# A graph layer in split single precision on one core: small tiles get a pool of their own ahead of the large ones

## The chip, the cores and the metric

The kernel runs on one core of one Trainium2 chip. The metric is the time of one execution in microseconds (us), as the device measures it; each kernel is run several times and the median counts.

## The reference

For each of 64 graphs with 256 nodes and 768 features the reference normalizes the features, takes the positive part `h`, and adds a graph layer to the input:

```python
h   = jnp.maximum(_layernorm(x, axis=-1), 0.0)
adj = heads.astype(hs.dtype);  radj = jnp.swapaxes(adj, 1, 2)
deg_c, rdeg_c = row sums of adj and radj, zeros replaced by 1
ctx = jnp.matmul(adj, hs @ Wadj.T + badj) / deg_c[..., None]
ctx = ctx + jnp.matmul(radj, hs @ Wrev.T + brev) / rdeg_c[..., None]
ctx = ctx + hs @ Wself.T + bself
rel = terms of the relation table E, gathered by adj and summed per node
out = x + ctx + rel
```

The heavy part is `h` (16,384 rows of 768) times three matrices of 768 x 768, and then the two aggregations with the adjacency matrix. All of it is in single precision.

## The kernel before

**The work.** The product of a graph's `h` with the three weight matrices is a product of a 2 x 3 by a 3 x 3 grid of blocks (two halves of the nodes, three parts of the features, three matrices). The kernel does it in 15 block products by fixed linear combinations (the tables `PRODUCTS` and `SWEEPS`), in two sweeps over the graphs: eight products (chains y, z and w) for all graphs first, then seven (chains x, v, u and t). Partial results go to DRAM between the sweeps. The first and the last graph are done with plain products (`whole`, L782).

**One product.** Its precision comes from splitting each operand into words of the format fp32r. The right operand (combined weights) is split once per sweep into three tiles `word{n}_0..2`, which stay in SBUF for all graphs. The left operand (a combination of parts of the transposed `h`) is split for each graph into one tile `left` of three words (`split`, L600 to L617). `passes` (L628) then issues matmuls of 128 x 128 by 384 columns: `left` is the stationary operand, loaded anew for each matmul, and `word` is the moving operand. A product has 12 such passes, in a run of eight and a run of four or the other way round, with a ScalarE operation on the PSUM bank between them (`scale`, L666). In the second sweep each graph also has four aggregations of eight passes (`aggregate`, L944), with `a` (the adjacency matrix) stationary and the pair `hl` (a block split in two words) moving.

**The order.** Nothing is ordered by hand. `record` writes down every operation with a rank, and `Plan.schedule` plays them through with estimated durations, engine by engine, and gives each buffer a slot of its class when it is first needed. The classes are W (24 slots of 6144 bytes in each partition: words, raw weights, `hl`), B (18 of 3072: `left`, `h`, blocks, rows), T (5 of 1024), A (3 of 4096: `adj`, `a`, some `x`), S (6 small ones: statistics, transposed statistics, diagonals), and Q and U in PSUM. The order and the slots come from the estimates alone; addresses play no part in them. Which slot a given `left`, `hl` or `a` gets changes from graph to graph.

**The addresses.** Each slot is one tag of the tile pool `pool`, and the pool lays its tags out in the order in which they first come up; a tag is as large as its largest tile, rounded up to 32 bytes. The constants end at byte 1248 of each partition. Then come, in the same pool, the tiles made by `own` (L1088): `deg` 1024 bytes, `sq` 512, two `cols` and two `tokens` of 512 each, two `rd` of 16. Then come the slots, in order of first use, so that S slots lie between W and B slots:

```
from byte  mod 256   what lies there
  1248       224     deg, sq, cols, tokens, rd
  4896        32     B B B W W
 26400        32     S (96 bytes), S (128 bytes)
 26624         0     W B A B W W B W W W
 76800         0     S (512 bytes), S (512 bytes)
 77824         0     B W W B B B B W W W B B W B W B W
154624         0     S (128 bytes)
154752       128     A B B A W B W W W W W W W
221312       128     S (512 bytes)
221824       128     T T T T T
226944               end
```

Within a tile the matmul operands start at multiples of 512 bytes from the tile's start.

The lines that the change touches are the definition of `own` (L1088) and the choice of a pool for a slot (L1109), both in `main_path`.

Of the kernel before, what the change touches and what calls it, by code (L numbers as in the profile page):

```python
# [1041 lines left out]
def kernel(  # L1042
# [34 lines left out]
    flag = const.tile([1, 1], I32, name="flag")  # L1077

    def main_path(main: ExitStack):
        pool = main.enter_context(tc.tile_pool(name="pool", bufs=1))  # L1080
        dram = main.enter_context(tc.tile_pool(name="dram", bufs=3, space=bass.MemoryType.DRAM))
        keep = main.enter_context(tc.tile_pool(name="kept", bufs=1, space=bass.MemoryType.DRAM))
        psum = main.enter_context(tc.tile_pool(name="psum", bufs=1, space=bass.MemoryType.PSUM))
        singles = ExitStack()
        single = singles.enter_context(tc.tile_pool(name="single", bufs=1, space=bass.MemoryType.PSUM))
        held, late = None, None
        plan = Plan(SLOTS)
        own = lambda name, shape, dtype: plan.buf(None, shape, dtype, name, pool.tile(shape, dtype, name=name))  # L1088
        fixed = {
            "x": x_v, "xt": x_t, "adj": adj_v, "out": out_v, "e_t": e_t, "bias": bias,  # L1090
            "w": (wadj_t, wself_t, wrev_t), "wr": (wr_t, wrr_t),
            "ident": ident, "ones": ones, "half": half, "dram": dram, "kept": keep,
            "flag": plan.buf(None, None, None, "flag", flag),
            "deg": own("deg", [P, B, C, 2], F32),
            "sq": own("sq", [P, B, C], F32),
            "cols": [own(f"cols{i}", [P, P], F32) for i in range(2)],
            "tokens": [own(f"token{i}", [P, P], F32R) for i in range(2)],
            "rd": [own(f"rd{i}", [P, C, 2], F32) for i in range(2)],
        }
        for col in fixed["cols"]:  # L1100
            nc.vector.memset(col.tile, 0.0)
        nc.scalar.activation(half[:, :1], half[:, :1], AF.Copy)
        record(nc, plan, fixed, B, NREL)
        for o in plan.schedule():
            for b in o.bufs:
                if b.name == "hold":
                    held = b.slot
                elif b.tile is None:
                    home = {"Q": psum, "U": single}.get(b.cls, pool)  # L1109
                    if b.cls == "Q" and b.slot == held:  # L1110
                        if late is None:
                            singles.close()
                            late = main.enter_context(tc.tile_pool(name="late", bufs=1, space=bass.MemoryType.PSUM))
                        home = late
                    b.tile = home.tile(b.shape, b.dtype, tag=f"{b.cls}{b.slot}", name=b.name)
            o.emit()
# [123 lines left out]
    with ExitStack() as main:  # L1240
        with tc.manual_schedule():
            main_path(main)
# [37 lines left out]
```

## Time and profile before

| | before |
|---|---|
| median of 3 runs | 2497.23 us (2497.17 to 2497.82) |
| the profiled execution | 2496.79 us |
| its span, first to last instruction | 2495.0 us |
| TensorE busy | 2468.1 us, 13,858 matmuls |
| VectorE, ScalarE, GpSimd busy | 2098.2, 1781.8, 1285.4 us |
| share of 16 DMA engines, main queue | 68.8% |

The profile is of one execution. Busy time is the union of an engine's instructions. A line number is that of the kernel before. A matmul's record lasts longer than its turn, since matmuls are pipelined: the pace of a run is read from its start to the start of what follows it.

### The profile page before, as it was taken

The page shows a single profiled execution, that of the slowest core. Times are in us where ns is not written, and L with a number is a line of the kernel's source. Part 1 is how long each engine was busy: PE and PEld are TensorE (multiplying, and loading weights), DVE is VectorE, ACT ScalarE, POOL GpSimd, SP SyncE. Part 2 cuts the span into 40 slices and gives each one's busy share as a digit, 9 for nine tenths or more (in the row PEclk, how much of TensorE's full clock was granted, in tenths as well). Part 3 has the DMA queues.
Part 4 walks back from the last instruction along what each step waited for, and adds up shares of the span by engine and source line. Part 5 has one row for each costly group of instructions (what it writes and reads, how often), then busy time and mean ns, then how long its engine had stood idle before and what let it go on. Part 6 is the DMA issues. An engine that isn't in the chain of part 4 may idle for free.

```text
span 2495.0 us, 43288 instructions
## 1 busy us (share of the span) xinstructions
PE 2468.1 (99%) x13858; PEld 2386.0 (96%) x13858; DVE 2098.2 (84%) x4003; ACT 1781.8 (71%) x3772; POOL 1285.4 (52%) x1138
## 2 busy tenths in 40 slices
PE   6999999999999999999999999999999999999999
PEld 4899999999999999996999999999999999999998
DVE  7887888788788778868988888888888888888887
ACT  4788888888888888876666666666666666666665
POOL 1555555555555555543555555555555555555554
PEclk9999999999999999999999999999999999999999
DMA  5677777777777777776666666666666666666663
GB/s 214 245 282 279 267 271 279 275 266 279 278 269 273 281 270 272 291 252 215 221 213 213 213 214 214 210 216 215 212 211 211 213 215 213 215 214 213 213 217 134
DMA packets 224776, 590.66 MB, mean 237 GB/s; under 512 B 25080, under 2 KB 25080, under 8 KB 224544
## 3 DMA queue, kind: packets, MB, share of 16 engines
q1 hardware_dynamic: 224544, 587.86, 68.8%
q8 instruction: 110, 1.80, 0.3%
q14 instruction: 122, 1.00, 0.1%
HBM read 364.28 MB, written 223.48 MB: 236 GB/s over the span
## 4 chain that ended last, share of the span: by engine, by line
PE 97%; DVE 1%; DMA 1%; ACT 1%; issue 0%; POOL 0%; SPq 0%; ACTq 0%; POOLq 0%
PE x L628 21%; PE y L628 20%; PE agg L944 14%; PE z L628 10%; PE w L628 10%; PE t L628 5%; PE v L628 5%; PE u L628 5%; PE whole L782 2%; PE v L638 1%; DMA raw<-in_Wself_dram 0%; PE right L502 0%; PE pt L915 0%; DMA row<-d 0%; DVE right L555 0%
## 5 line engine op out<-in xcount | busy, mean ns | idle before, releaser
L932 POOL TENSOR_TENSOR hl<-c,hl 128x768 fp32r<-128x768 f32 x256 | 476.0, 1860 | 655.4 <-ACT hl L928 449.6
L628 PE MATMUL x<-word,left 128*128 128x384 f32 x2976 | 592.1, 340 | 0.2 <-DVE c L687 0.2
L628 PE MATMUL y<-word,left 128*128 128x384 f32 x2976 | 573.9, 337 | 0.1
L628 PEld LDWEIGHTS x<-word,left 128*128 128x128 f32 x2976 | 517.5, 188 | 14.1 <-issue 11.2
L628 PEld LDWEIGHTS y<-word,left 128*128 128x128 f32 x2976 | 522.9, 188 | 4.1 <-ACT y L666 1.0
L944 PE MATMUL agg<-hl,a 128*128 128x384 f32 x2048 | 399.1, 337 | 0.0
L944 PEld LDWEIGHTS agg<-hl,a 128*128 128x128 f32 x2048 | 361.9, 188 | 0.5 <-issue 0.2
L745 POOL TENSOR_TENSOR h<-h,row 128x768 f32<-128x768 f32 x128 | 235.2, 1859 | 172.5 <-DMA row<-d 138.6
L628 PE MATMUL z<-word,left 128*128 128x384 f32 x1488 | 301.3, 337 | 0.7 <-DVE x L793 0.4
L628 PE MATMUL w<-word,left 128*128 128x384 f32 x1488 | 301.5, 338 | 0.2 <-ACT w L666 0.2
L666 ACT ACTIVATE x<-x 128x768 f32<-128x768 f32 x248 | 191.8, 794 | 141.5 <-PE x L628 141.5
L628 PEld LDWEIGHTS w<-word,left 128*128 128x128 f32 x1488 | 264.1, 188 | 0.8 <-ACT w L666 0.7
L628 PEld LDWEIGHTS z<-word,left 128*128 128x128 f32 x1488 | 260.6, 188 | 3.8 <-DVE x L793 0.7
L955 DVE SCALAR_TENSOR_TENSOR c<-agg,rd,c 128x768 f32<-128x768 f32 x252 | 255.2, 1013 | 8.5 <-PE agg L944 4.2
L928 ACT ACTIVATE hl<-c 128x768 fp32r<-128x768 f32 x256 | 215.1, 841 | 30.3 <-DVE c L685 24.4
L666 ACT ACTIVATE y<-y 128x768 f32<-128x768 f32 x248 | 197.0, 794 | 42.4 <-PE y L628 41.4
L722 POOL TENSOR_TENSOR cols<-cols,half 128x2 f32<-128x2 f32 x64 | 83.1, 1298 | 259.3 <-DVE cols L721 259.3
L617 DVE SCALAR_TENSOR_TENSOR left<-left,top 128x256 fp32r<-128x256 f32 x496 | 199.8, 414 | 6.4
L685 DVE TENSOR_TENSOR c<-c,v 128x768 f32<-128x768 f32 x124 | 117.4, 947 | 104.2 <-PE v L628 103.2
L617 DVE SCALAR_TENSOR_TENSOR left<-left 128x256 fp32r<-128x256 f32 x434 | 203.8, 492 | 0.1
L607 ACT ACTIVATE top<-left 128x256 f32<-128x256 f32 x496 | 180.8, 382 | 6.2 <-DVE left L617 2.1
L676 ACT ACTIVATE c<-y 128x768 f32<-128x768 f32 x124 | 100.9, 814 | 72.2 <-PE y L628 72.1
(136 smaller groups left out, 4320.1 us busy)
## 6 DMA issues: line engine op xcount, KB each, us to landing
c<-kept SPq DMA_DIRECT2D x316, 384.0 KB
kept<-c SPq DMA_DIRECT2D x252, 384.0 KB
x<-in_x_dram SPq DMA_DIRECT2D x128, 384.0 KB
h<-in_x_t_dram SPq DMA_DIRECT2D x128, 384.0 KB
out_dram<-c SPq DMA_DIRECT2D x126, 384.0 KB
kept_h<-h SPq DMA_DIRECT2D x124, 384.0 KB
h<-kept_h SPq DMA_DIRECT2D x124, 384.0 KB
adj<-in_adj_dram SPq DMA_DIRECT2D x64, 512.0 KB
```

The costliest lines, as they stand in the source:

```text
L607: lambda: nc.scalar.activation(view(top), t(w)[:, 0].bitcast(F32), AF.Copy),
L617: lambda: nc.vector.scalar_tensor_tensor(t(w)[:, 2], t(w)[:, 1].bitcast(F32), -STEP, first(), op0=ALU.mult, op1=ALU.add), s == 1,
L628: nc.tensor.matmul(t(q)[:, half, : H // 2], t(w)[:, lw, f, :], t(r[rw])[:, f, ts(half, H // 2)], start=start and i == 0 and f == 0, stop=s ...
L666: lambda: nc.scalar.activation(view(), view(), AF.Copy, scale=scale),
L676: lambda o=o, sign=sign: nc.scalar.activation(t(o).rearrange("p (k n) -> p k n", k=2), view(), AF.Copy, scale=sign * (1.0 if value_last el ...
L685: emit = lambda to=to, op=op: nc.vector.tensor_tensor(to(), to(), view(), op=op)
L722: pool(0.7, r - 21.5, f"pow {b}", [col], [col], lambda: nc.gpsimd.tensor_tensor(var(), var(), v["half"], op=ALU.pow))
L745: lambda h=h, one=one: nc.gpsimd.tensor_tensor(t(h), t(h), one(0), op=ALU.subtract),
L928: lambda: nc.scalar.activation(t(pair)[:, 0], t(o), AF.Copy, scale=LOWER),
L932: lambda: nc.gpsimd.tensor_tensor(t(pair)[:, 1], t(o), t(pair)[:, 0].bitcast(F32), op=ALU.subtract),
L944: nc.tensor.matmul(t(q)[:, half, : H // 2], t(s["a"])[:, c, k, ts(ic, P)], t(pairs[c])[:, part, ts(half, H // 2)], start=(c == 0 and part ...
L955: lambda q=q, to=to, ic=ic: nc.vector.scalar_tensor_tensor(to(), t(q)[:, :, : H // 2], t(rd)[:, ic, k : k + 1], to(), op0=ALU.mult, op1=AL ...
```

## The change

The tiles made by `own` and the S slots come from a second pool, `small`, which is opened ahead of `pool` and so lies ahead of it in each partition. Sizes, slots, operations and their order are the same.

```diff
     def main_path(main: ExitStack):
+        small = main.enter_context(tc.tile_pool(name="small", bufs=1))
         pool = main.enter_context(tc.tile_pool(name="pool", bufs=1))
...
-        own = lambda name, shape, dtype: plan.buf(None, shape, dtype, name, pool.tile(shape, dtype, name=name))
+        own = lambda name, shape, dtype: plan.buf(None, shape, dtype, name, small.tile(shape, dtype, name=name))
...
                 elif b.tile is None:
-                    home = {"Q": psum, "U": single}.get(b.cls, pool)
+                    home = {"Q": psum, "U": single, "S": small}.get(b.cls, pool)
```

## Rows read from the trace of the kernel before

**Rows 1.** The page, head and part 1: busy us, share of the span, instructions

```profile
span 2495.0 us, 43288 instructions
...
PE 2468.1 (99%) x13858; PEld 2386.0 (96%) x13858; DVE 2098.2 (84%) x4003; ACT 1781.8 (71%) x3772; POOL 1285.4 (52%) x1138
```

**Rows 2.** The page, part 4: the chain that ended last, share by engine

```profile
PE 97%; DVE 1%; DMA 1%; ACT 1%; issue 0%; POOL 0%; SPq 0%; ACTq 0%; POOLq 0%
```

**Rows 3.** Waits of TensorE: us in total, times, longest us

```profile
PE whole L782 <- DVE h L749: 18.9, 1, 18.9
PE pt L915 <- DVE x L793: 0.8, 1, 0.8
PE z L628 <- DVE x L793: 0.4, 1, 0.4
PE t L628 <- ACT t L666: 0.2, 1, 0.2
PE x L628 <- DVE c L687: 0.2, 1, 0.2
PE z L628 <- ACT z L666: 0.2, 1, 0.2
PE w L628 <- ACT w L666: 0.2, 1, 0.2
```

**Rows 4.** Busy time by stretch: first sweep, second sweep (columns in the first line)

```profile
core 0: us, PE busy (x) PEld busy (x) DVE busy (x) ACT busy (x) POOL busy (x), PEclk, DMA share, GB/s
100.00:1050.00 950.00, 949.92 (x5419) 945.96 (x5418) 759.99 (x1692) 796.59 (x1585) 525.12 (x511) 1.00 0.77 275
1200.00:2430.00 1230.00, 1230.00 (x7089) 1202.67 (x7089) 1086.31 (x1878) 793.69 (x1822) 642.34 (x529) 1.00 0.66 214
```

**Rows 5.** Groups by line, matmuls: xcount | busy us, mean ns | idle before

```profile
L628 PE MATMUL x<-word,left 128*128 128x384 f32 x2976 | 592.1, 340 | 0.2 <-DVE c L687 0.2
L628 PE MATMUL y<-word,left 128*128 128x384 f32 x2976 | 573.9, 337 | 0.1
...
L944 PE MATMUL agg<-hl,a 128*128 128x384 f32 x2048 | 399.1, 337 | 0.0
...
L628 PE MATMUL w<-word,left 128*128 128x384 f32 x1488 | 301.5, 338 | 0.2 <-ACT w L666 0.2
L628 PE MATMUL z<-word,left 128*128 128x384 f32 x1488 | 301.3, 337 | 0.7 <-DVE x L793 0.4 <-ACT z L666 0.2
...
L628 PE MATMUL t<-word,left 128*128 128x384 f32 x744 | 151.1, 338 | 0.2 <-ACT t L666 0.2
L628 PE MATMUL u<-word,left 128*128 128x384 f32 x744 | 150.7, 337 | 0.0
L628 PE MATMUL v<-word,left 128*128 128x384 f32 x744 | 150.2, 337 | 0.0
...
L782 PE MATMUL whole<-raw,h 128*128 128x384 f32 x288 | 97.3, 493 | 18.9 <-DVE h L749 18.9
```

**Rows 6.** Timeline of TensorE, two successive graphs: start us, us, what

```profile
1552.06 1.56 PE L944 MATMUL agg<-hl,a 128*128 128x384 f32 x8
1553.47 0.85 PE L628 MATMUL x<-word,left 128*128 128x384 f32 x4
1554.16 1.58 PE L628 MATMUL t<-word,left 128*128 128x384 f32 x8
1555.58 1.21 PE L628 MATMUL x<-word,left 128*128 128x384 f32 x6
...
1573.08 1.55 PE L944 MATMUL agg<-hl,a 128*128 128x384 f32 x8
1574.47 0.85 PE L628 MATMUL x<-word,left 128*128 128x384 f32 x4
1575.16 1.57 PE L628 MATMUL t<-word,left 128*128 128x384 f32 x8
1576.57 1.21 PE L628 MATMUL x<-word,left 128*128 128x384 f32 x6
```

**Rows 7.** Timeline of TensorE, the run of u in two graphs

```profile
1502.38 1.55 PE L628 MATMUL u<-word,left 128*128 128x384 f32 x8
1503.77 0.86 PE L628 MATMUL v<-word,left 128*128 128x384 f32 x4
...
1565.37 1.57 PE L628 MATMUL u<-word,left 128*128 128x384 f32 x8
1566.78 0.86 PE L628 MATMUL v<-word,left 128*128 128x384 f32 x4
```

**Rows 8.** Timeline of TensorE, runs of z and w in the first sweep

```profile
502.89 0.86 PE L628 MATMUL z<-word,left 128*128 128x384 f32 x4
503.59 1.57 PE L628 MATMUL w<-word,left 128*128 128x384 f32 x8
505.00 1.22 PE L628 MATMUL y<-word,left 128*128 128x384 f32 x6
...
519.73 0.87 PE L628 MATMUL z<-word,left 128*128 128x384 f32 x4
520.44 1.04 PE L628 MATMUL w<-word,left 128*128 128x384 f32 x5
...
1008.34 1.55 PE L628 MATMUL w<-word,left 128*128 128x384 f32 x8
1009.73 1.03 PE L628 MATMUL y<-word,left 128*128 128x384 f32 x5
```

## The prediction

> **What bounds the kernel.** I read the page's busy times first: TensorE is busy 2468.1 us of a span of 2495.0 us, 99%, and VectorE, the next, 84% [rows 1]. The reader is to see there that one engine fills the span. The chain of waits then has to confirm that this engine also sets the end, and it does: 97% of the chain is TensorE [rows 2]. The list of what TensorE waited for shows the slack in that: 18.9 us once, at the start, and less than 1 us for every other entry [rows 3]. The table by stretches says the same of the two long stages: TensorE is busy 949.92 of 950 us in the first (batches through the first sweep of products) and 1230.00 of 1230 us in the second, at a granted clock of 1.00, the 2.4 GHz level, while VectorE has 760 and 1086 us [rows 4]. So the time is a number of matmuls times the pace of one.
>
> How many: L628 issues 2976 + 2976 + 1488 + 1488 + 744 + 744 + 744 = 11,160 and L944 issues 2048, together 13,208 passes of 384 columns [rows 5]. How fast: the first stage has 949.92 us / 5419 = 175.3 ns for one [rows 4], and over the 12,923 of these passes that follow another one without a gap, start to start in the timeline, it is 175.2 ns. One nanosecond more or less in each is 13.2 us, half a per cent of the span. A change that only moves tiles can act here and nowhere else.
>
> **The change part by part.** It adds no instruction, wait or transfer, and takes none away: the same tiles get other addresses in each partition. By the tile sizes, the old pool starts at byte 1248; the named small tiles take 3648 bytes (1024 + 512 + 4 x 512 + 2 x 32), so the large ones begin at 4896, which is 32 modulo 256. The six S slots (96, 128, 512, 512, 128 and 512 bytes) lie among the large ones and move what follows: tiles from 4896 on have remainder 32, from 26,624 on 0, from 154,752 on 128. W, B, A and T tiles are all multiples of 1024 bytes. After the change the S slots, 1888 bytes, stand ahead, the large tiles begin at 4896 + 1888 = 6784, and every one has remainder 128. The two tokens keep 224; the pool's end stays where it is.
>
> With the program's addresses I sorted the 13,208 passes by the difference, modulo 256, between the moving operand (word or hl) and the stationary one (left or a): 5628 have none, 4712 have 128, 1044 have 96 or 160, 1824 have 32 or 224. After the change all have none. The price of a difference is read by comparing one and the same run of matmuls in two batches in which the plan put its stationary tile into different slots, from its start to the start of the next row:
> - L944, last run of a batch, eight passes, hl at 0. At 1552.06 us with a at 128: 1.41 us; at 1573.08 with a at 0: 1.39 [rows 6]. These alternate; over 31 batches of each kind the means are 1.405 and 1.394 (1.391 without one run that was held up), 1.4 to 1.8 ns a pass.
> - u, eight passes, words at 128. At 1502.38 with left at 128: 1.39; at 1565.37 with left at 0: 1.41 [rows 7]. All five batches with equal remainders have 1.39 (mean 1.392), 42 with left at 0 have 1.409: 2.2 ns a pass. Here 128 against 128 takes the lower value.
> - z, four passes, word at 0: 502.89 with left at 0, 0.70; 519.73 with left at 128, 0.71; and w, eight passes, words at 128: 503.59 with left at 0, 1.41; 1008.34 with left at 128, 1.39 [rows 8]. Regular batches have z at 0.697 (26 with left at 0), 0.705 (23 at 128) and 0.699 (10 at 32).
>
> Not every place answers so strongly: runs whose words are mixed, as t below, gain on one half what they lose on the other. Over all places of L628 and L944, each measured against its own passes with equal remainders, a difference of 128 costs 1.44 ns, 96 or 160 cost 1.2, and 32 or 224 are 0.7 cheaper than none. The sum:
> - 128 removed: 4712 x 1.44 = 6.8 us gained
> - 96 and 160 removed: 1044 x 1.2 = 1.2 us gained
> - 32 and 224 removed: 1824 x 0.7 = 1.3 us lost
>
> That is 6.7 us. Fitting all differences at once, with a level for each place, gives 5.8 us with an uncertainty of 1.6. I take 6.3. For the ends: with the strongest run, 2.2 ns for 128, the sum is 10.4 + 1.2 - 1.3 = 10.3; with 0.8 ns, half a weak place, 3.8 + 1.2 - 1.3 = 3.7.
>
> The Trainium skill speaks against this. Its page "TensorE: Matmul & The Clock Gate", section "Step-by-step: what each phase is for", says that TensorE has two independent read ports, one for the streaming operand and one for weight loads, and that "Loading the next tile's weights doesn't steal SBUF read bandwidth from the running matmul". By that rule the sum would be 0. The runs above do not agree with it to the last 1%: 1.41 against 1.39.
>
> **What else moves, at nothing.** The token rows (L638) have tokens at 224 against rows at 0, and afterwards rows at 128; the two-pass matmuls (L782, 288 passes of 493 ns mean [rows 5]) go from mixed to equal. Neither has a comparison of its own in the trace, so I bound them by 2.2 ns a pass either way: 256 and 288 passes, 0.6 us each. I take 0. VectorE, ScalarE and GpSimd also get new addresses. Cover: VectorE's least slack is 1230 - 1086 = 144 us in the second stage and 190 in the first [rows 4], 12% and 20%; 6.3 us less of TensorE takes 0.3% of it. A gain there is worth nothing, a loss under a tenth too. Waits of TensorE outside the start are about 2 us in all [rows 3], so little of the gain can be given back; I take 0, at most 1 us.
>
> **The rivals.**
> - *Nothing that can be measured.* The differences in the runs are due to what other engines do in those batches, not to addresses. For it: the a slots alternate with the batch, as much else does, and t shows 1.42 us at 1554.16 and 1.41 at 1575.16 with its left at 0 both times [rows 6], so some pace moves without addresses. Against: u's five batches at 1.39 don't alternate, and z and w of another stage show the same [rows 7, 8]. The time would be 2497.2, within 1 us. This is also what the rule of the Trainium skill would make of it.
> - *Remainder 128 is itself slow (the other side).* Every stretch above that takes the upper value has an operand at 128; if that and not the difference costs, all passes go at w's 1.41 / 8 = 176.3 ns [rows 8] in place of 175.2: 13,208 x 1.1 = 14.5 us more, 2511.7. It decides as soon as equal operands at 128 run over 175.5 ns (1.404 for eight). Against: u at 1502.38 and w at 1008.34 have both operands at 128 and take the lower value [rows 7, 8].
> - *More than the sum.* If weak places owe their level to differences with their neighbours, which are never equal in this program, the strongest price holds everywhere: 10.3 us, 2486.9. For it: some places of w and y have no batch with equal remainders, so their level is unknown.
>
> **How the numbers follow.** The profiled execution took 2496.79 us, span 2495.0 and 1.8 around it; 2496.79 - 6.3 = 2490.5. The median of the runs, 2497.23, is 0.44 above it, so I predict 2490.9. About 0.2%, 5 us, is what can be told from no change: faster means under 2492.2. My forecast, a saving of 3.7 to 9 us, has 0.71; its uncertainty of 2 us puts 0.58 of that below 2492.2 and 0.13 above. The empty rival has 0.16, remainder 128 0.05, the large one 0.08. Faster is 0.58 + 0.08 = 0.66, same 0.13 + 0.16 = 0.29, slower 0.05. The range, 2486.5 to 2496, takes in the forecast and most of the large gain (which ends at 2486.9), and leaves out some of the empty rival and all of the one on the other side.
>
> **What would show it.** Right: L944's last run and u's eight passes take 1.39 us in every batch, z's four 0.70; the passes in the first stage's stretch come to about 174.8 ns; the same order of instructions and 2 us of waits. Half right: those runs even out while t and x keep 1.41. Wrong: u and L944 alike at 1.41 (128 is slow), or alternating as before (addresses do nothing), or a new entry of several us among TensorE's waits.

## The result and the profile after

The changed kernel takes 2478.49 us, median of six runs (2476.78 to 2479.24), against 2497.2 of the kernel before beside it: a ratio of 0.9924, 95% interval 0.9911 to 0.9937. That is 18.7 us faster. The forecast was 2490.9 with a range of 2486.5 to 2496, so the sign was right and the size three times too small.

The page of the changed kernel, head, busy times and the engines' shares of the chain:

```profile
span 2476.5 us, 43288 instructions
...
PE 2449.1 (99%) x13858; PEld 2365.0 (95%) x13858; DVE 2096.0 (85%) x4003; ACT 1777.2 (72%) x3772; POOL 1283.1 (52%) x1138
...
PE 97%; DVE 1%; DMA 1%; ACT 1%; issue 0%; POOL 0%; SPq 0%; ACTq 0%; POOLq 0%
```

The same instructions, TensorE 19 us less busy, the others within 5 us of before [rows 1], the chain as before [rows 2]. What TensorE waited for after, as in [rows 3] (us in total, times, longest):

```profile
PE whole L782 <- DVE h L749: 18.9, 1, 18.9
PE pt L915 <- DVE x L793: 1.1, 1, 1.1
PE z L628 <- DVE x L793: 0.4, 1, 0.4
```

No wait has come or gone. All of it is pace. Busy time by stretch after, with the columns of [rows 4]:

```profile
core 0: us, PE busy (x) PEld busy (x) DVE busy (x) ACT busy (x) POOL busy (x), PEclk, DMA share, GB/s
100.00:1050.00 950.00, 949.90 (x5467) 944.29 (x5466) 767.27 (x1709) 800.85 (x1596) 528.60 (x514) 1.00 0.77 278
1200.00:2410.00 1210.00, 1210.00 (x7031) 1182.79 (x7030) 1074.60 (x1863) 784.13 (x1801) 634.96 (x523) 1.00 0.67 216
```

The first stage goes from 175.3 ns a matmul [rows 4] to 949.90 / 5467 = 173.75; the granted clock is 1.00 in both, the 2.4 GHz level. The foretold runs, in the same graphs as [rows 6] to [rows 8]; timeline of TensorE after (start us, us, what):

```profile
500.58 1.55 PE L628 MATMUL w<-word,left 128*128 128x384 f32 x8
501.97 0.51 PE L628 MATMUL y<-word,left 128*128 128x384 f32 x2
...
1540.89 1.55 PE L944 MATMUL agg<-hl,a 128*128 128x384 f32 x8
1542.27 0.85 PE L628 MATMUL x<-word,left 128*128 128x384 f32 x4
1542.97 1.55 PE L628 MATMUL t<-word,left 128*128 128x384 f32 x8
1544.35 0.51 PE L628 MATMUL x<-word,left 128*128 128x384 f32 x2
...
1554.06 1.55 PE L628 MATMUL u<-word,left 128*128 128x384 f32 x8
1555.45 0.86 PE L628 MATMUL v<-word,left 128*128 128x384 f32 x4
...
1561.71 1.55 PE L944 MATMUL agg<-hl,a 128*128 128x384 f32 x8
1563.09 0.68 PE L628 MATMUL x<-word,left 128*128 128x384 f32 x3
```

From its start to the next row every run of eight takes 1.38 or 1.39 us: w (1.41 before, [rows 8]), L944 in both graphs, u (1.41 before, [rows 7]). And t, whose left lay at 0 in both graphs of [rows 6], falls from 1.42 and 1.41 to 1.38.

**Where the 18.7 us come from.** The order of instructions is the same, so each pass of 384 columns that another one follows without a gap (12,918 of them) can be set against itself, from its start to the start of the next. Sorted by the difference that it had in the kernel before:

```
difference  passes   gained each   together
128          4614     2.50 ns      11.55 us
96            781     2.10          1.64
160           247     1.52          0.38
224          1230     0.81          1.00
32            563    -0.38         -0.22
none         5483     0.97          5.33
all else (waits, two-pass matmuls, passes beside token rows)  -1.0
```

The last line but one is the one that the forecast didn't have: passes whose operands were equal before and are equal after gained 5.3 us.

The gain goes with the pass's own pair of operands more than with the weights that come next: of the passes with equal operands, 268 had a difference of 128 between their moving operand and the stationary operand of the pass behind them, and these gained nothing (0.0 ns each); 252 with 128 in their own pair and none to the next one's stationary operand gained 2.9 ns each. Other combinations are fewer and less even.

### The profile page after: what moved, and what is told of

Its sections match the earlier page's. It is cut to its first block, busy times and chain, and to the rows that moved or that the text cites. A ratio compares the mean times of both kernels' runs of the same rounds, so it can differ in the third digit from the quotient of the medians.

```text
span 2476.5 us, 43288 instructions
## 1 busy us (share of the span) xinstructions
PE 2449.1 (99%) x13858; PEld 2365.0 (95%) x13858; DVE 2096.0 (85%) x4003; ACT 1777.2 (72%) x3772; POOL 1283.1 (52%) x1138
## 4 chain that ended last, share of the span: by engine, by line
PE 97%; DVE 1%; DMA 1%; ACT 1%; issue 0%; POOL 0%; SPq 0%; ACTq 0%; POOLq 0%
PE x L628 21%; PE y L628 21%; PE agg L944 14%; PE z L628 10%; PE w L628 10%; PE t L628 5%; PE v L628 5%; PE u L628 5%; PE whole L782 2%; PE v L638 1%; DMA raw<-in_Wself_dram 0%; PE right L502 0%; PE pt L915 0%; DMA row<-d 0%; DVE right L555 0%
## 5 line engine op out<-in xcount | busy, mean ns | idle before, releaser
L628 PE MATMUL x<-word,left 128*128 128x384 f32 x2976 | 589.3, 339 | 0.2 <-DVE c L687 0.2
L628 PE MATMUL y<-word,left 128*128 128x384 f32 x2976 | 569.3, 335 | 0.0
L628 PEld LDWEIGHTS x<-word,left 128*128 128x128 f32 x2976 | 515.2, 188 | 14.2 <-issue 11.0
L628 PEld LDWEIGHTS y<-word,left 128*128 128x128 f32 x2976 | 517.8, 188 | 5.2 <-ACT y L666 1.0
L944 PE MATMUL agg<-hl,a 128*128 128x384 f32 x2048 | 395.3, 334 | 0.0
L944 PEld LDWEIGHTS agg<-hl,a 128*128 128x128 f32 x2048 | 358.4, 188 | 0.6 <-issue 0.2
L628 PE MATMUL z<-word,left 128*128 128x384 f32 x1488 | 299.3, 335 | 0.7 <-DVE x L793 0.4
L628 PE MATMUL w<-word,left 128*128 128x384 f32 x1488 | 298.2, 334 | 0.2 <-ACT w L666 0.2
L628 PEld LDWEIGHTS z<-word,left 128*128 128x128 f32 x1488 | 258.7, 188 | 4.5 <-DVE x L793 0.7
L628 PEld LDWEIGHTS w<-word,left 128*128 128x128 f32 x1488 | 261.3, 188 | 0.8 <-ACT w L666 0.5
```

The costliest lines, as they stand in the source:

```text
L628: nc.tensor.matmul(t(q)[:, half, : H // 2], t(w)[:, lw, f, :], t(r[rw])[:, f, ts(half, H // 2)], start=start and i == 0 and f == 0, stop=s ...
L944: nc.tensor.matmul(t(q)[:, half, : H // 2], t(s["a"])[:, c, k, ts(ic, P)], t(pairs[c])[:, part, ts(half, H // 2)], start=(c == 0 and part ...
```

## The experiments

Differences are moving minus stationary operand, modulo 256, unless said. Every run keeps the kernel's arithmetic and order; only addresses differ. Each is timed against the kernel before, and the changed kernel was run once more in the series (2478.84).

**Level or difference, price in full, and neighbours.** Four kernels from the changed one. The first adds a pad of 128 bytes ahead of all large tiles, which puts them at remainder 0; the second and third put the W slots (the words and hl, the moving operands) into a pool of their own behind a pad of 128 or 64 bytes, so that all 13,208 passes have that difference; the fourth moves one B slot (a stationary tile) by 128.

```diff
+        small.tile([P, 32], F32, name="pad")
```

```diff
+        wide = main.enter_context(tc.tile_pool(name="wide", bufs=1))
+        wide.tile([P, 32], F32, name="pad")
...
-                    home = {"Q": psum, "U": single, "S": small}.get(b.cls, pool)
+                    home = {"Q": psum, "U": single, "S": small, "W": wide}.get(b.cls, pool)
```

(16 in place of 32 for 64 bytes.)

```diff
+        odd = main.enter_context(tc.tile_pool(name="odd", bufs=1))
+        odd.tile([P, 32], F32, name="pad")
...
+                    if b.cls == "B" and b.slot == 16:
+                        home = odd
```

> The changed kernel with 128 unused bytes ahead of the large tiles, so that all of them have remainder 0 modulo 256 in place of 128. Theory A (only the difference between the two operands counts, and a pass with unequal operands also delays the equal passes behind it): same time as the changed kernel, 2478.5 us within 1.5, and 173.6 ns a pass. Rival B (remainder 128 itself is good, which would explain why the gain was three times the sum): most of the 12.4 us beyond the forecast is lost, 2485 to 2491 us, 174.3 ns or more a pass.

> The changed kernel with the 24 W slots (words and hl, the moving operands) in a pool of their own behind the others and 128 bytes further, so that all 13,208 passes have a difference of 128 and none changes from one to the next. Theory A: the kernel before shows 176.1 ns a pass in stretches of five and more passes with that difference, against 173.6 now: 13,208 x 2.5 = 33 us more, 2511 us, slower than the kernel before. Price of the prediction (1.44 ns for each such pass, nothing else): 2478.5 + 19 = 2497.5. Rival C (what costs is the change of remainder from pass to pass, not the difference): 2478.5.

> The same with 64 bytes in place of 128: all passes have a difference of 64 (192 the other way), which the kernel before does not contain. In the kernel before, stretches of passes with a difference of 32 or 224 run at 173.3 to 173.8 ns, and with 96, 128 or 160 at 176 to 177. If the cost begins between 32 and 64: about 176 ns and 2505 to 2515 us. If between 64 and 96: 173.6 ns and 2478.5 us. No theory decides this ahead; I lean to the cost (0.6).

> The changed kernel with one of the 18 B slots displaced by 128 bytes (it holds the left operand of about 50 of the 930 block products, 600 of 13,208 passes). Theory A: these 600 passes take about 176 ns, and the passes behind each run of them, though equal, 175.9, 175.4, 175.3, 174.3, 173.8 and then 173.4 ns, as in the kernel before: 1.5 us for the passes themselves and 0.6 us behind them, 2480.5 us. Price of the prediction: the passes behind such a run are at 173.4 ns from the first one on. The time alone can't tell these apart; the timeline behind the runs can.

Measured: all at 0, 2478.10 us (ratio 0.9920, 0.9904 to 0.9937); words at 128, 2508.43 (1.0043, 1.0026 to 1.0060); words at 64, 2476.91 (0.9914, 0.9898 to 0.9931); one slot, 2479.30 (0.9924, 0.9908 to 0.9941). So the remainder itself doesn't count. A difference of 128 held by every pass costs 2508.43 - 2478.5 = 29.9 us, or 29.9 / 13,208 = 2.3 ns a pass, not the 1.44 of the forecast, by which the time would have been 2497.5. A difference of 64, where I leaned to a cost, costs nothing. Stretch of the first stage, columns as in [rows 4], words at 128, then words at 64:

```profile
100.00:1050.00 950.00, 949.93 (x5401) 946.23 (x5400) 757.51 (x1689) 793.59 (x1577) 524.20 (x509) 1.00 0.77 274
```

```profile
100.00:1050.00 950.00, 949.90 (x5471) 944.26 (x5470) 767.57 (x1710) 800.55 (x1596) 530.76 (x514) 1.00 0.78 279
```

66 matmuls fewer in the same 950 us than after's 5467, or 4 more: that is the whole difference. In the kernel with words at 128 the run of u takes 1.40 us in both graphs (timeline of TensorE):

```profile
1507.84 1.56 PE L628 MATMUL u<-word,left 128*128 128x384 f32 x8
1509.24 0.52 PE L628 MATMUL v<-word,left 128*128 128x384 f32 x2
...
1571.18 1.56 PE L628 MATMUL u<-word,left 128*128 128x384 f32 x8
1572.58 0.69 PE L628 MATMUL v<-word,left 128*128 128x384 f32 x3
```

The one slot gives 591 passes a difference, which cost 2.1 ns each there (175.8 against 173.7 in the changed kernel), and the equal passes behind them are slower too: 1.45, 0.89, 0.49 and 0.28 ns for the first to the fourth. That is a tail on neighbours, weaker than the one of the kernel before.

**Half of the words, and 32.** Odd W slots alone in the padded pool (pad of 8 or 32 floats), so that differences alternate; all words at 32; and words at 64 with the tokens and cols in the large pool, so that the token rows and the transposes have equal operands (the two runs of this are called "64 with tokens moved" below).

```diff
+        wide.tile([P, 8], F32, name="pad")
...
+                    if b.cls == "W" and b.slot % 2:
+                        home = wide
```

```diff
+        even = lambda name, shape, dtype: plan.buf(None, shape, dtype, name, pool.tile(shape, dtype, name=name))
...
-            "tokens": [own(f"token{i}", [P, P], F32R) for i in range(2)],
+            "tokens": [even(f"token{i}", [P, P], F32R) for i in range(2)],
```

> The changed kernel with every second W slot 32 bytes further: 5992 of 13,208 passes have a difference of 32, the rest none, and the difference changes 809 times from 0 to 32 and 865 times back. In the kernel before, held against the same passes of the changed kernel, stretches with a difference of 32 or 224 cost nothing by themselves, but the equal stretch behind one is 14 ns (behind 32) to 21 ns (behind 224) longer in all. Theory A2 (a change of the difference disturbs the passes behind it, whatever the passes cost): 865 x 14 = 12 us less 809 x 2.7 = 2 us, 2488.5 us. Theory A1 (only unequal passes cost, by their difference): 2478 us. Price of the prediction (0.7 ns cheaper than equal ones): 2474 us.

> The same with 128 bytes in place of 32: 5992 passes with a difference of 128, the same 809 and 865 changes. By the stretches of the kernel before (14.5 ns for a stretch that begins with a change from 0 to 128, 4.9 ns more in the equal stretch behind it): 11.7 + 4.2 = 16 us, 2494.5 us. By half of what all passes at 128 cost (30.3 us): 5992 / 13,208 x 30.3 = 13.7 us, 2492 us. Price of the prediction: 5992 x 1.44 = 8.6 us, 2487 us.

> The changed kernel with all W slots 32 bytes further, so that all 13,208 passes have a difference of 32 and it never changes. Theories A1 and A2: 2477 to 2478.5 us, as with 0 and 64, since stretches with 32 cost nothing by themselves. If a difference of 32 costs like 128: 2508 us.

> The version with a difference of 64 throughout (2476.9 us), and besides the two tokens and the two cols tiles in the large pool, so that the token rows and the transposes have equal operands too (they had 96 or 160). The passes behind these two places are the ones still above 175 ns in the second sweep; if their operands' difference causes that, 1 to 2 us less, 2475.5 us; if it is the short matmuls themselves, 2476.9 us.

Measured: half at 32, 2483.34 (0.9941, 0.9924 to 0.9958); half at 128, 2496.05 over ten runs (0.9989, 0.9980 to 0.9999); all at 32, 2488.07 (0.9958, 0.9944 to 0.9973); 64 with tokens moved, 2475.72 (0.9909, 0.9893 to 0.9926). All at 32, which I expected to cost nothing, costs 9.6 us, 0.72 ns a pass. Half at 128 (5992 passes) costs 17.6 us, 3.8 us more than 5992 x 2.3 = 13.8. Put down to its 1674 changes between one difference and another, these 3.8 us are some 2.3 ns for each. Half at 32 costs 4.8 us, 0.5 more than 5992 x 0.72, or 0.3 ns for each change; none of the three times set for it (2488.5, 2478 and 2474) was met.

Half at 32 shows who pays. Its passes with a difference of 32 take 173.35 ns, the same ones in the changed kernel 173.52: by their own rows they look free. The equal passes behind them pay: the first 175.04 (173.64 in the changed kernel), the second 178.59 (173.49), the rest little. A run of z of eight equal passes behind such a stretch (timeline; half at 32, then the changed kernel):

```profile
963.86 1.58 PE L628 MATMUL z<-word,left 128*128 128x384 f32 x8
965.28 1.55 PE L628 MATMUL y<-word,left 128*128 128x384 f32 x8
```

```profile
963.21 1.55 PE L628 MATMUL z<-word,left 128*128 128x384 f32 x8
964.61 1.72 PE L628 MATMUL y<-word,left 128*128 128x384 f32 x9
```

1.42 against 1.40 us, with equal operands in both.

**Without the second pool, and 96.** First the kernel before with fill tiles behind three of the S slots (40, 32 and 32 floats), nothing else moved: all large tiles get remainder 32 and the small ones stay among them. Then all words at 96 (the pad of 24 floats), the changed kernel again, and 64 with tokens moved again.

```diff
+                    fill = {0: 40, 1: 32, 4: 32}.get(b.slot) if b.cls == "S" else None
+                    if fill and b.slot not in filled:
+                        filled.add(b.slot)
+                        pool.tile([P, fill], F32, name=f"fill{b.slot}")
```

> The kernel before, with its small tiles where they were, and unused bytes behind the S slots of 96, 128 and 128 bytes that fill each up to 256. All large tiles then have remainder 32. If equal remainders are the whole of the change: as the changed kernel, 2478 us within 1.5. If it is where the small tiles lie (ahead of the large ones): 2497 us.

> The changed kernel with all W slots 96 bytes further, so that all passes have a difference of 96. The kernel before shows 175.6 to 177 ns in stretches with 96, as much as with 128 (2508 us when all passes have it): 2505 to 2515 us. But short stretches misjudged 32 (they showed no cost; all passes at 32 cost 10 us), so anything from 2488 up is open; below 2485 would say that the cost comes from 128 alone.

> The changed kernel itself, beside the next one on the same chip, as the measure for it: 2478.3 us.

> The version with a difference of 64 throughout and the tokens and cols tiles in the large pool, again, beside the changed kernel: 2475.7 us against 2478.3, 0.1% faster. If the 2.6 us between their earlier medians are between chips or calls, no difference.

Measured: filled, 2480.42 (0.9930, 0.9915 to 0.9945); words at 96, 2516.13 (1.0074, 1.0058 to 1.0089); the changed kernel again, 2478.84 (0.9922, 0.9909 to 0.9936); 64 with tokens moved again, 2475.72 (0.9909, 0.9894 to 0.9924). First stage of the filled kernel, then of words at 96:

```profile
100.00:1050.00 950.00, 949.90 (x5470) 944.43 (x5469) 766.77 (x1710) 800.56 (x1595) 528.42 (x514) 1.00 0.77 278
```

```profile
100.00:1050.00 950.00, 949.95 (x5377) 946.79 (x5377) 754.72 (x1681) 789.59 (x1569) 520.79 (x505) 1.00 0.77 274
```

Equal remainders alone, by 416 bytes of fill, bring nine tenths of the gain; where the small tiles lie is not what counts. The 1.6 to 1.9 us by which the filled kernel stays above the changed one lie behind the transposes (L915) and the token rows (L638): the 1369 passes that are among the twelve behind one of these take 1.6 us more than in the changed kernel, the third of the twelve 184.7 ns in place of 175.1, and all other passes take 0.3 us less. Why just these, no run shows. 96 costs 2.85 ns a pass, the most of all, and is just above the 2505 to 2515 us expected. The tokens bring nothing that shows: the two kernels with tokens moved have a pace of 173.46 and 173.42 ns, words at 64 alone 173.48. Against the changed kernel in the same series, 2475.72 and 2478.84 are 0.1% apart with ranges that touch. The traces show where 64 is ahead of 0: in the same 1369 passes the three kernels at 64 take 1.3, 1.6 and 1.6 us less than the changed kernel, whose second execution differs there from its first by 0.0. Far from these places a difference of 0 and one of 64 have the same steady pace, 173.3 ns.

**Does the sign count?** Words at 160 and at 224, which are 96 and 32 the other way round (pads of 40 and 56 floats).

> The changed kernel with all W slots 160 bytes further, so that all passes have a difference of 160. If the cost depends on the distance in the 256 bytes alone (96 one way is 160 the other way): 2516 us, as with 96. If the direction counts: the kernel before has 247 such passes at 175.9 ns, 1.5 ns above the changed kernel's: 2498 us.

> The same with 224 bytes. By distance alone: 2488 us, as with 32. If the direction counts: the 1230 passes of the kernel before with 224 are 0.8 ns above the changed kernel's, but the equal passes behind them 20 ns a stretch: 2489 to 2500 us. At 2478.5 a difference of 224 would cost nothing and the bill of these stretches would lie in the changes alone.

Measured: 2476.28 (0.9913, 0.9897 to 0.9930) and 2478.51 (0.9920, 0.9904 to 0.9937): both free. Both of the times that I had set for 160, 2516 and 2498, were wrong. First stage with words at 160:

```profile
100.00:1050.00 950.00, 949.90 (x5472) 944.34 (x5471) 767.58 (x1711) 800.54 (x1596) 528.60 (x514) 1.00 0.77 278
```

5472 against 5377 for 96: it matters which operand lies ahead.

**Is the period 256?** Words at 384, 352 and 288, which are 128, 96 and 32 modulo 256 (pads of 96, 88 and 72 floats).

> The changed kernel with all W slots 384 bytes further. 384 is 128 modulo 256, and the other form in which the kernel before has that difference (2012 passes with 384 modulo 512, 2700 with 128). If 256 bytes is the period, as the change has it: 2508 us, as with 128. If 512 is: open; the kernel before has both forms at 176.0 ns, so about 2508 all the same.

> The same with 352 bytes, 96 modulo 256; all 796 passes of the kernel before with 96 have this form modulo 512. Period 256: 2516 us, as with 96. Period 512: the kernel before has these passes at 175.6 ns against 173.5, 2505 us.

> The same with 288 bytes, 32 modulo 256; all 564 passes of the kernel before with 32 have this form modulo 512. Period 256: 2488 us, as with 32. Period 512: the kernel before has these passes at 173.4 ns, below the changed kernel's 173.8, so 2478 us, and what they cost would lie in the changes alone.

Measured: 2509.12 (1.0039, 1.0025 to 1.0053), 2516.76 (1.0073, 1.0056 to 1.0090), 2488.09 (0.9959, 0.9944 to 0.9973). Each is within 0.7 us of its fellow with 256 bytes less. The period is 256. The filled kernel says the same of equal operands: by its addresses 5756 of its passes are 256 apart modulo 512, and away from the transposes and token rows they take 173.5 ns, as the same passes of the changed kernel do.

## Why the prediction was too small

- **The bound was right.** TensorE's pace was the only thing that moved; waits stayed at their 2 us and the order the same. The other engines' addresses cost nothing that shows in TensorE's waits, and the terms taken at nothing stayed small: the token rows took the same time, the two-pass matmuls 0.4 us more, where two executions of the changed kernel differ by 1.0.
- **The direction was right, and the runs named for it did what was foretold**: L944's last run, u's and w's eight at 1.39 in all batches but one each of L944 and w that were held up, z's four at 0.693. The pace of the first stage, foretold at 174.8 ns, is 173.75.
- **The step that failed** is "Over all places of L628 and L944, each measured against its own passes with equal remainders". It took the equal passes of the kernel before as undisturbed. They were not: by their place behind the last pass with a difference they took 176.2, 175.6, 175.4, 174.0 ns for the first to the fourth and 173.9 for the fifth to the seventh, and only the eighth 173.5; after the change 173.9, 174.0, 173.6, 173.6 and 173.3 to 173.4. So the baseline held part of the price. It shrank 128 to 1.44 (2.3 in full), and it made 32 and 224 look cheaper than equal passes. In the terms of the forecast's sum, by the table of the 18.7 us: 128 brought 11.6 us in place of 6.8; 96 and 160 brought 2.0 in place of 1.2; 32 and 224 gained 0.8 where 1.3 was to be lost; and the equal passes, which the sum left out, gained 5.3. A run of t with words and left both at 0 shows the tail; timeline of the kernel before, behind a stretch with a difference of 224:

```profile
1515.66 0.88 PE L628 MATMUL t<-word,left 128*128 128x384 f32 x4
1516.38 0.87 PE L628 MATMUL x<-word,left 128*128 128x384 f32 x4
```

The same run after:

```profile
1504.78 0.85 PE L628 MATMUL t<-word,left 128*128 128x384 f32 x4
1505.47 0.85 PE L628 MATMUL x<-word,left 128*128 128x384 f32 x4
```

0.72 against 0.69 us for four equal passes. Before, ten batches with a 224 stretch ahead have a mean of 0.716, 28 with an equal stretch ahead 0.693. I could have read this before the change was built: sorting equal passes by what ran ahead of them needs only the old trace.
- **The sum with measured prices.** 128: 4712 x 2.3 = 10.8 us. 96: 796 x 2.85 = 2.3. 32: 564 x 0.72 = 0.4, a gain where the forecast had a loss. 160 and 224: nothing. Together 13.5. Grouping 96 with 160 and 32 with 224 was wrong as well, since one of each pair is free. The other 5.2 us can be put down to the places where the kernel before changes from one difference to another, 2070 times (which is argued from the half kernels, not measured by itself); at the 0.3 to 2.3 ns a change that the two half kernels show, this is 0.6 to 4.7 us, so 14.1 to 18.2 of 18.7 are accounted for. That the remainder closes only with the upper price, that of 128 and none in turn (991 of the 2070), is left standing.
- **The rivals.** "Nothing that can be measured" and "remainder 128 is itself slow" fell: equal operands at 128, at 0 and at 32 (changed, all at 0, filled) have one pace, 173.6 to 173.7 ns. "More than the sum" had the right mechanism, weak places that owe their level to their neighbours, with a chance of 0.08. It was mis-sized too, because it kept 32 and 224 as a loss and gave the equal passes themselves nothing to gain.
- **Of the Trainium skill**, page "TensorE: Matmul & The Clock Gate", section "Step-by-step: what each phase is for": that weight loads don't take read bandwidth from the running matmul fits the differences 0, 64, 160 and 224, where the time is 2476 to 2479 us. It can't be the whole account, since with the same instructions 32, 96 and 128 take 2488, 2516 and 2508.

What is left open: why these three cost and the others don't (no run looks into the path of the operands), 192 (not tried), and up to 4.6 us of the sum, by the price that a change of difference is given.

## What to carry to other kernels

Where back-to-back matmuls with a weight load each are the bound, compute both operands' addresses modulo 256 for every pass and bring the difference to 0 throughout (64, 160 and 224 did as well here; a constant 96 or 128 is slower than the mixture of the kernel before); small tiles of odd sizes between large ones are what breaks it, and a few hundred bytes of fill mend it. When a price is read by comparing runs inside one trace, first ask whether the cheap runs are undisturbed: sort them by what ran ahead of them, and take as baseline only those far behind the last disturbed one. Two things that look symmetric (96 and 160) are two prices until a run shows one.

## What the runs showed of the hardware

All of it was seen with one kind of matmul: 128 x 128 by 384 columns of fp32r words, new weights for each, at a granted clock of 1.00; other widths and formats were not tried. The price of a difference depends on its sign and repeats every 256 bytes. Time and mean ns of a back-to-back pass of 384 columns, when every pass has the same difference:

```
difference      0       32      64      96      128     160     224
time, us        2478.5  2488.1  2476.9  2516.1  2508.4  2476.3  2478.5
+256, us                2488.1          2516.8  2509.1
ns per pass     173.6   174.4   173.5   176.6   176.0   173.5   173.6
```

Under the means lie fixed rhythms. Successive starts of equal passes are 173, 173, 174 ns apart and so on, which is 173.3, or 416 cycles at 2.4 GHz for 384 columns. With 128 they run 174, 175, 182, 176, 173 and again from the start (176.0), with 96 175, 178, 174, 180 (176.8), with 160 as with none.

With 32 there are two rhythms at one and the same difference: some stretches run 175, 172, 175, 172 (with a 171 now and then, a mean of 173.3), as cheap as none, and others 175, 180, 174, 178 (176.7), as dear as 96. About seven tenths of the passes go at the one and under three tenths at the other, so the 174.4 of the table is a mean of two paces. The same runs of two successive graphs, words at 32 (timeline of TensorE):

```profile
1509.24 1.55 PE L628 MATMUL t<-word,left 128*128 128x384 f32 x8
1510.62 2.24 PE L628 MATMUL x<-word,left 128*128 128x384 f32 x12
...
1530.15 1.57 PE L628 MATMUL t<-word,left 128*128 128x384 f32 x8
1531.57 2.28 PE L628 MATMUL x<-word,left 128*128 128x384 f32 x12
```

The run of t takes 1.38 us in the one graph and 1.42 in the other. So a short stretch that looks free doesn't show that its difference is. What decides between the two paces was not looked at.

In the changed kernel 606 passes still take over 175 ns. 248 of them are among the twelve behind a transpose or the token rows, and with words at 160 only 41 are left there. 350 are in the first sweep, where there is neither between the runs, most of them in z's run of eight and where w gives way to y. What these owe was not settled.
